# A graph layer on one core: the first block's outer products in two fp32r parts, other rings of buffers, gelu's table loaded at another place

## The chip, the cores and the metric

The kernel runs on one core of a Trainium2 chip. The core has five engines that run side by side, each through its own list of instructions in order: TensorE (PE in the profile; its weight loads are PEld), VectorE (DVE), ScalarE (ACT), GpSimd (POOL) and SyncE (SP), which here only issues transfers. They wait for each other by semaphores. On-chip memory is SBUF, matmuls add up in PSUM, and the DMA engines move data between SBUF and the memory outside (DRAM). The metric is the device time of one execution in microseconds (us), lower is better, as the median of several runs.

## The reference

There are 625 nodes with 512 features and 20,625 edges (10,000 in both directions, and a loop at each node), sorted by destination. An edge has a source, a destination, one of four relation types and a weight.

```python
h   = relu(layernorm(x))
msg = sum over r: (h[src] @ W_rel[r] + b_rel[r]) * (weight where type == r, else 0)
agg = segment_sum(msg, dst) / max(segment_sum(weight, dst), 1)
x1  = layernorm(h + h @ W_self + b_self + agg) * g1 + b1
ffn = gelu(x1 @ W_ffn1 + b_ffn1) @ W_ffn2 + b_ffn2      # 512 -> 1024 -> 512
out = x + layernorm(x1 + ffn) * g2 + b2
```

All inputs are fp32.

## The kernel before

**Tiles.** The nodes, padded to 640, form five blocks of 128. The edges form 162 tiles of 128. As edges are sorted by destination, a tile's edges fall in one block, or in two where blocks meet; `EdgePlan` works out which, with bounds that hold for nearly every graph. Edges outside of those bounds are counted (`count_outside`), and a branch at the end repeats the work in another way if there are any.

**First stage.** For each relation r and block i, `table_rows` multiplies the normalized block by `W_rel[r]` (L199), VectorE adds the bias (L202), and the rows are written to a table in DRAM, 2,560 rows in all. `later_loads` brings the other weights. VectorE prepares columns of the edge list and one-hot tiles for the degree sums (`degree_hots`). The order of TensorE, VectorE and ScalarE in this stage is the one written.

**Gathered tiles.** After that stage `edge_tile` handles the 132 tiles that touch blocks 1 to 4. GpSimd gathers the 128 table rows of the tile's edges into `ms` (L484). ScalarE multiplies them by the weights and rounds to the type fp32r, which gives `hi` (L489); VectorE computes the rest, `lo` (L491). TensorE multiplies each by a one-hot of the destinations and adds them up in PSUM (L507, L508): two matmuls of type fp32r in place of one in fp32. A one-hot tile serves four edge tiles (L503). `ms` has a ring of `MS = 13` buffers, `hi` and `lo` one of three each.

**First block.** The 36 tiles that touch block 0 gather nothing. `first_sums` takes two at a time. A one-hot `os` of the source's row in its chunk (L285) is multiplied, as an outer product over the tile's edges, by `od`: a matrix that holds the edge's weight in the column of its destination and chunk (L291, compare and multiply in one instruction). L300 adds the products up in PSUM banks, in fp32, 58 products of 20 to 420 columns; when a bank is complete, ScalarE copies it to `sums_w` (L305). `first_products` then multiplies these sums by the table itself: SyncE loads it in 20 chunks of 128 rows, `tr` (L363), and L374 multiplies, two chunks a step. `tr` uses the same ring as `ms`, and a load is issued `LA = 4` chunks ahead.

**Degree, self part, norm, feed-forward.** `degree_sums` adds up the weights of each node, `degree_end` inverts them and sends them through DRAM to turn them into columns (`rdeg`), with two transfers on SP's queue. `self_part` is `h @ W_self` of a block (L210), kept in DRAM too. When a block's sum is complete, `first_norm` runs on VectorE, the block is transposed by TensorE (L180), `up` multiplies by `W_ffn1` in eight pieces with gelu on ScalarE (L401, L403), `down` multiplies by `W_ffn2` (L409), and the second norm and the store follow.

**Order.** From the second stage on, TensorE's order comes from a planner in the program: it keeps a clock of its own, places a gathered tile whenever one is due (the first at 7.5 us, then one each 1.33), and between them takes the offered step of lowest rank whose due time has come: degree sums 0, the first block's work 1, other self parts 2, a transpose 9, feed-forward 10. Each step carries an estimated length; a transpose is due 9 us after its block's norm has been placed. The order on the other engines is left to the scheduler. `total_outside` is the matmul that adds up the count of edges outside (L249) and the copy of the count (L250).

Of the kernel before, what the change touches and what calls it, by code (L numbers as in the profile page):

```python
# [42 lines left out]
def gnn_layer(ctx, tc, x, edges, w_self, w_rel, w_ffn1, w_ffn2, rows_in, bf1_in, out, n_edges):  # L43
# [89 lines left out]
    ones = const.tile([P, 1], F32, name="ones")  # L133
    nc.vector.memset(ones, 1.0)
    half = const.tile([P, 1], F32, name="half")
    nc.vector.memset(half, -0.5)
# [129 lines left out]
    def first_columns():  # L266
# [11 lines left out]
                                       op0=ALU.mult, op1=ALU.add)  # L278

    bank = {}  # L280

    def first_sums(j0, n):

        oh = work.tile([P, 2, P], F32, tag="os", name=f"os_{j0}")
        nc.vector.tensor_tensor(oh[:, :n, :], key[:, 0, j0:j0 + n].unsqueeze(2).to_broadcast([P, n, P]),  # L285
                                node_row[:, :P].unsqueeze(1).to_broadcast([P, n, P]), op=ALU.is_equal)
        for j in range(j0, j0 + n):
            lo, hi = ep.window[j]
            hi = min(hi, P)
            ow = work.tile([P, NW * NC], F32, tag="od", name=f"od_{j}", bufs=3)  # L290
            nc.vector.tensor_scalar(ow[:, :(hi - lo) * NC], key_row[:, :(hi - lo) * NC], key[:, 1, j:j + 1],  # L291
                                    wgt[:, j:j + 1], op0=ALU.is_equal, op1=ALU.mult)
            for q in range(lo // BW, (hi - 1) // BW + 1):
# [6 lines left out]
                nc.tensor.matmul(bank[q][:, (a - q * BW) * NC:(z_ - q * BW) * NC], oh[:, j - j0, :],  # L300
                                 ow[:, (a - lo) * NC:(z_ - lo) * NC],
                                 start=False, stop=(j == meets[-1]))
                if j == meets[-1]:
# [75 lines left out]
    def first_norm(b, agg, pool_pow=False):  # L379
        zi = z[:, b, :]  # L380
        nc.vector.scalar_tensor_tensor(zi, agg, rdeg[:, b:b + 1], zi, op0=ALU.mult, op1=ALU.add)
        mean, t = variance(zi, f"z{b}")
        a = work.tile([P, D], F32, tag="hn", name=f"za_{b}")
        nc.vector.scalar_tensor_tensor(a, zi, mean, g1_bc, op0=ALU.subtract, op1=ALU.mult)
        rstd = rsqrt_pow(t, True) if pool_pow else rsqrt_scaled(t)
        x1 = work.tile([P, D], F32, tag="x1", name=f"x1_{b}")
        nc.vector.scalar_tensor_tensor(x1, a, rstd, b1_bc, op0=ALU.mult, op1=ALU.add)
# [4 lines left out]
    def feed_forward(blocks, x1T, gT, pool_pow=False):  # L392
# [12 lines left out]
        def down(i, f):  # L405
# [5 lines left out]
            if f + 2 < KF:  # L411
                return
            y = work.tile([P, D], F32, tag="y", name=f"y_{i}")
            nc.vector.tensor_add(y, po[i], z[:, i, :])
            mean, t = variance(y, f"y{i}")
            a = work.tile([P, D], F32, tag="hn", name=f"ya_{i}")
            nc.vector.scalar_tensor_tensor(a, y, mean, g2_bc, op0=ALU.subtract, op1=ALU.mult)
# [13 lines left out]
    DG = 27  # L431
    MS = 13
    LA = 4
    chunks = [(j0, min(DG, NT - j0)) for j0 in range(0, NT, DG)]
    groups = [(j0, min(2, n_first - j0)) for j0 in range(0, n_first, 2)]
    with tc.manual_schedule(engines={PE, DVE, ACT}):
# [13 lines left out]
        for r in range(R):  # L450
            for i in range(NB):
# [21 lines left out]
    with tc.manual_schedule(engines={PE}):  # L473
# [7 lines left out]
        def edge_tile(j):  # L481
# [5 lines left out]
            w = wgt[:, j:j + 1]  # L487
            hi = edge.tile([P, D], F32R, tag="hi", name=f"hi_{j}")
            nc.scalar.activation(hi, ms, AF.Copy, scale=w)  # L489
            lo = edge.tile([P, D], F32R, tag="lo", name=f"lo_{j}")  # L490
            nc.vector.scalar_tensor_tensor(lo, ms, w, hi.bitcast(F32), op0=ALU.mult, op1=ALU.subtract)  # L491
# [42 lines left out]
        def norm_and_feed(b):  # L534
# [13 lines left out]

            offer(9, now + 9.0, [(0.7, 0.0, turned)])

# [25 lines left out]
        while left or steps:  # L576
# [18 lines left out]
    with tc.If(some_out > 0):  # L595
# [4 lines left out]
        with tc.For_i(0, NT, 1) as j:  # L600
# [4 lines left out]
            nc.vector.tensor_copy(gw[:, 1:2], wgt[:, bass.ds(j, 1)])  # L605
            gm = work.tile([P, D], F32, tag="y", name="gm")
            nc.gpsimd.indirect_dma_start(
# [57 lines left out]
```

## Time and profile before

| | |
|---|---|
| runs | 330.9, 331.29, 334.62 us; median 331.29 |
| profiled execution | 366.07 us, of which the span between its first and last instruction is 364.2 |
| TensorE's granted clock, mean | 0.929 |
| TensorE busy | 301.1 us, 83% of the span |
| VectorE busy | 229.0 us, 63% |
| GpSimd busy | 153.1 us, 42% |
| ScalarE busy | 120.9 us, 33% |
| moved by DMA | 61.71 MB, 169 GB/s over the span |

A profile comes from one execution, and this one took longer than the plain runs. Times in it are microseconds from the span's start. "Busy" counts an engine's instructions; a matmul's end is modelled and overlaps the next one, so that the distance from start to start tells more of TensorE than the length of one. An fp32 matmul leaves two records, one of type fp32r leaves one, and both are printed with the output's type f32. In a group of instructions, "idle before" is the time for which the engine stood still ahead of them, with what released it. The chain of waits is followed back from the last instruction, at each step to what released it.

### The profile page before, as it was taken

How to read it: one execution, taken by the hardware profiler on the slowest of the kernel's cores; microseconds unless marked ns; L12 is line 12 of the kernel's file. 1: busy time of each engine (PE TensorE's matmuls, PEld its weight loads, DVE VectorE, ACT ScalarE, POOL GpSimd, SP SyncE). 2: the span in 40 equal slices, each digit the busy share in tenths (PEclk: the TensorE clock that was granted, in tenths of full speed). 3: DMA queues.
4: the chain of work that ended last, by engine and by line, in shares of the span. 5: the costliest groups of instructions: out<-in, count | busy, mean ns of one | idle time of the engine just before them, and what ended most of it. 6: DMA issues, size and time to landing. Idle time of an engine off the chain costs nothing.

```text
span 364.2 us, 4077 instructions
## 1 busy us (share of the span) xinstructions
PE 301.1 (83%) x1264; PEld 191.1 (52%) x1266; DVE 229.0 (63%) x470; ACT 120.9 (33%) x195; POOL 153.1 (42%) x224
## 2 busy tenths in 40 slices
PE   1799999997847599999988947398989975999990
PEld 0344444445523468775544426285776665687750
DVE  2324767995623579998675561398757866786503
ACT  2230000000330345653433432364545525562210
POOL 5100000001777437743444777367757774301001
PEclk9999999999878599999989997699998996999997
DMA  7989852121877455575688667355656674400000
GB/s 281 413 298 335 281 190 86 58 86 61 167 198 253 142 163 147 170 225 161 213 302 282 174 200 202 94 150 173 185 158 187 174 207 124 146 2 30 6 28 27
DMA packets 24556, 61.71 MB, mean 169 GB/s; under 512 B 4577, under 2 KB 4577, under 8 KB 24274
## 3 DMA queue, kind: packets, MB, share of 16 engines
q0 software_dynamic: 10560, 34.61, 33.2%
q1 hardware_dynamic: 13968, 26.79, 20.8%
q8 instruction: 12, 0.20, 0.2%
q14 instruction: 14, 0.11, 0.1%
q10 hardware_dynamic: 2, 0.00, 0.0%
HBM read 53.55 MB, written 7.84 MB: 169 GB/s over the span
## 4 chain that ended last, share of the span: by engine, by line
PE 58%; issue 11%; DMA 9%; DVE 8%; another core or an unknown queue 5%; ACT 5%; POOL 2%; SPq 0%; POOLq 0%; ACTq 0%; DVEq 0%
PE pt L199 19%; PE po L409 8%; PE pu L401 7%; PE acc L508 7%; PE acc L507 6%; DMA ms<-table,row_i 6%; PE bank L300 5%; PE pz L210 4%; ACT hi L489 4%; DVE lo L491 4%; POOL ms L484 2%; DMA xs<-in_x_dram 2%; PE acc L374 1%; DMA table<-m 1%
## 5 line engine op out<-in xcount | busy, mean ns | idle before, releaser
L484 POOL DMA_INDIRECT ms<-table,row_i x132 | 143.3, 1085 | 151.2 <-issue 91.2
L489 ACT ACTIVATE hi<-ms,ed 128x512 fp32r<-128x512 f32 x132 | 92.5, 719 | 157.8 <-DMA ms<-table,row_i 95.4
L491 DVE SCALAR_TENSOR_TENSOR lo<-ms,ed,hi 128x512 fp32r<-128x512 f32 x132 | 96.9, 747 | 58.6 <-ACT hi L489 36.4
L507 PE MATMUL acc<-hi,oh 128*128 128x512 f32 x150 | 80.1, 534 | 19.9 <-issue 10.7
L199 PE MATMUL pt<-wr,hT 128*128 128x512 f32 x160 | 71.0, 603 | 0.0
L508 PE MATMUL acc<-lo,oh 128*128 128x512 f32 x150 | 64.9, 432 | 6.1 <-DVE lo L491 5.6
L401 PE MATMUL pu<-x1T,w_sb 128*128 128x128 f32 x320 | 44.7, 289 | 7.2 <-issue 6.5
L199 PEld LDWEIGHTS pt<-wr,hT 128*128 128x128 f32 x160 | 30.8, 195 | 37.4 <-issue 36.9
L401 PEld LDWEIGHTS pu<-x1T,w_sb 128*128 128x128 f32 x320 | 44.3, 205 | 10.8 <-issue 6.9
L507 PEld LDWEIGHTS acc<-hi,oh 128*128 128x128 f32 x150 | 30.5, 203 | 33.9 <-issue 18.6
L508 PEld LDWEIGHTS acc<-lo,oh 128*128 128x128 f32 x150 | 30.4, 202 | 24.3 <-DVE lo L491 13.8
L409 PE MATMUL po<-w_sb,gT 128*128 128x512 f32 x80 | 36.6, 592 | 0.0
L503 DVE TENSOR_TENSOR oh<-fl,node_row 128x512 fp32r<-128x512 f32 (+2 forms) x39 | 25.5, 666 | 8.3 <-DMA table<-m 3.2
L202 DVE TENSOR_TENSOR m<-pt,brel_bc 128x512 f32<-128x512 f32 x20 | 13.7, 688 | 23.2 <-PE pt L199 23.2
L300 PE MATMUL bank<-od,os 128*128 128x60 f32 (+19 forms) x116 | 27.0, 369 | 0.6 <-issue 0.6
L403 ACT ACTIVATE gT<-pu,bf 128x128 f32<-128x128 f32 x40 | 14.7, 367 | 36.6 <-PE pu L401 15.5
L300 PEld LDWEIGHTS bank<-od,os 128*128 128x128 f32 x116 | 21.6, 214 | 4.5 <-issue 0.9
L409 PEld LDWEIGHTS po<-w_sb,gT 128*128 128x128 f32 x80 | 14.9, 189 | 13.4 <-issue 12.5
L374 PE MATMUL acc<-tr,sums_w 128*128 128x512 f32 x40 | 20.0, 625 | 0.0
L210 PE MATMUL pz<-ws_sb,hT 128*128 128x512 f32 x40 | 19.2, 624 | 0.0
L291 DVE TENSOR_SCALAR od<-key_row,key,ed 128x400 f32<-128x400 f32 (+15 forms) x36 | 15.7, 443 | 0.8 <-PE bank L300 0.8
L210 PEld LDWEIGHTS pz<-ws_sb,hT 128*128 128x128 f32 x40 | 8.4, 211 | 8.2 <-issue 7.8
(94 smaller groups left out, 161.9 us busy)
## 6 DMA issues: line engine op xcount, KB each, us to landing
table<-m SPq DMA_DIRECT2D x20, 256.0 KB
tr<-table SPq DMA_DIRECT2D x20, 256.0 KB
wr<-in_L_gnn_W_rel_dram SPq DMA_DIRECT2D x4, 1024.0 KB
w_sb<-in_L_gnn_W_ffn_dram SPq DMA_DIRECT2D x2, 2048.0 KB
ms<-table,row_i POOLq DMA_INDIRECT x132
rows<-in_rows_dram SPq DMA_DIRECT2D x1, 1536.0 KB
z_kept<-z SPq DMA_DIRECT2D x5, 256.0 KB
xs<-in_x_dram SPq DMA_DIRECT2D x2, 512.0 KB
```

The lines of the kernel that those rows point to most:

```text
L199: nc.tensor.matmul(p, hT[:, k, i * P:(i + 1) * P], wr_sb[r][:, k, :], start=(k == 0), stop=(k == KD - 1))
L210: nc.tensor.matmul(p, hT[:, k, i * P:(i + 1) * P], ws_sb[:, k, :], start=(k == 0), stop=(k == KD - 1))
L300: nc.tensor.matmul(bank[q][:, (a - q * BW) * NC:(z_ - q * BW) * NC], oh[:, j - j0, :], ow[:, (a - lo) * NC:(z_ - lo) * NC], start=False, s ...
L374: nc.tensor.matmul(acc[0], sums_w[:, c_, :], chunks_[c_], start=(c_ == 0), stop=(c_ == NC - 1))
L401: nc.tensor.matmul(pu[:, :nn], w1_sb[:, k, f * P:(f + 1) * P], x1T[:, k, n0:n0 + nn], start=(k == 0), stop=(k == KD - 1))
L409: nc.tensor.matmul(po[i], g[:, f_, i * P - n0:(i + 1) * P - n0], w2_sb[:, f_, :], start=(f_ == 0), stop=(f_ == KF - 1))
L484: nc.gpsimd.indirect_dma_start(out=ms, out_offset=None, in_=table[:, :], in_offset=bass.IndirectOffsetOnAxis(ap=row_i[:, j:j + 1], axis=0))
L489: nc.scalar.activation(hi, ms, AF.Copy, scale=w)
L491: nc.vector.scalar_tensor_tensor(lo, ms, w, hi.bitcast(F32), op0=ALU.mult, op1=ALU.subtract)
L503: nc.vector.tensor_tensor(ohs[b][:, :ng, :], dst_f[:, j:j + ng].unsqueeze(2).to_broadcast([P, ng, P]), node_row[:, b * P:(b + 1) * P].unsq ...
L507: nc.tensor.matmul(acc[b], oh, hi, start=first, stop=False)
L508: nc.tensor.matmul(acc[b], oh, lo, start=False, stop=end)
```

## The change

- **Outer products.** `os` is multiplied by the weights in place of `od`. The weight is split into an fp32r part and the rest (`first_weights`, two small instructions on VectorE in the first stage). ScalarE scales each `os` tile by either part into `ohw` (two activations of 128 columns for each of the 36 tiles, 72 in all), `od` is a comparison alone, written as fp32r, and each product becomes two fp32r matmuls, one for each part, into the same bank. `ohw` and `od` share the ring of six that the degree one-hots (`oc`) had.
- **Rings.** `MS` goes from 13 to 7, `hi` gets five buffers and `lo` four. `tr` has a ring of its own with three buffers, and `LA` goes from 4 to 3. The tiles of both norms move to the ring of six of the degree stage's `ow`.
- **gelu's table.** An activation of one column with Gelu is placed in the first stage, after relation 0, and brings the table load with it.
- **Planner.** The transfer that brings `rdeg` and the count of edges outside (`total_outside`) are steps of their own, due at 14 us of the planner's clock. The transposes of all blocks but the last are due 15 us after the norm, not 9.

In the order of the built program the count's matmul leaves the head of TensorE's second stage and comes behind seven gathered tiles; the outer products have fewer gathered tiles and one self part fewer between them, and these follow later. On SP the first three `tr` loads stand ahead of the two degree transfers and the stores of the self part.

```diff
+    w2 = const.tile([P, 2, n_first], F32R, name="w2")
+
+    def first_weights():
+        nc.vector.tensor_copy(w2[:, 0, :], wgt[:, :n_first])
+        nc.vector.tensor_sub(w2[:, 1, :], wgt[:, :n_first], w2[:, 0, :].bitcast(F32))
...
         oh = work.tile([P, 2, P], F32, tag="os", name=f"os_{j0}")
+        ohw = work.tile([P, 2, 2, P], F32R, tag="oc", name=f"ohw_{j0}", bufs=6)
...
-            ow = work.tile([P, NW * NC], F32, tag="od", name=f"od_{j}", bufs=3)
+            for part in range(2):
+                nc.scalar.activation(ohw[:, j - j0, part, :], oh[:, j - j0, :], AF.Copy,
+                                     scale=w2[:, part, j:j + 1].bitcast(F32))
+            ow = work.tile([P, NW * NC], F32R, tag="oc", name=f"od_{j}", bufs=6)
             nc.vector.tensor_scalar(ow[:, :(hi - lo) * NC], key_row[:, :(hi - lo) * NC], key[:, 1, j:j + 1],
-                                    wgt[:, j:j + 1], op0=ALU.is_equal, op1=ALU.mult)
+                                    None, op0=ALU.is_equal)
...
-                nc.tensor.matmul(bank[q][:, (a - q * BW) * NC:(z_ - q * BW) * NC], oh[:, j - j0, :],
-                                 ow[:, (a - lo) * NC:(z_ - lo) * NC],
-                                 start=False, stop=(j == meets[-1]))
+                for part in range(2):
+                    nc.tensor.matmul(bank[q][:, (a - q * BW) * NC:(z_ - q * BW) * NC], ohw[:, j - j0, part, :],
+                                     ow[:, (a - lo) * NC:(z_ - lo) * NC],
+                                     start=False, stop=(j == meets[-1] and part == 1))
...
         nc.sync.dma_start(deg_dram.rearrange("(a c) -> c a", c=C), dg[:, 0, :])
+
+    def degree_rows():
         nc.sync.dma_start(rdeg, deg_dram.rearrange("(b p) -> p b", p=P))
...
-            tr = edge.tile([P, D], F32, tag="ms", name=f"tr_{c}", bufs=MS)
+            tr = edge.tile([P, D], F32, tag="tr", name=f"tr_{c}", bufs=LA)
...
-    MS = 13
-    LA = 4
+    MS = 7
+    HL = 5
+    LA = 3
...
                 if r == 0 and i == NB - 1:
+                    nc.scalar.activation(gelu_of, ones, AF.Gelu)
                     first_columns()
+                    first_weights()
...
-            hi = edge.tile([P, D], F32R, tag="hi", name=f"hi_{j}")
+            hi = edge.tile([P, D], F32R, tag="hi", name=f"hi_{j}", bufs=HL)
...
-            lo = edge.tile([P, D], F32R, tag="lo", name=f"lo_{j}")
+            lo = edge.tile([P, D], F32R, tag="lo", name=f"lo_{j}", bufs=HL - 1)
...
-            offer(9, now + 9.0, [(0.7, 0.0, turned)])
+            offer(9, now + (9.0 if last else 15.0), [(0.7, 0.0, turned)])
...
+        offer(-1, 14.0, [(0.0, 0.0, degree_rows), (0.2, 0.0, total_outside)])
...
                     degree_end(pdeg)
-                    total_outside()
                     did = True
```

More of the change, by code (lines that the diff above doesn't have):

```diff
@@ L134, in gnn_layer @@
     nc.vector.memset(ones, 1.0)
+    gelu_of = const.tile([P, 1], F32, name="gelu_of")
     half = const.tile([P, 1], F32, name="half")
@@ L382, in first_norm @@
         mean, t = variance(zi, f"z{b}")
-        a = work.tile([P, D], F32, tag="hn", name=f"za_{b}")
+        a = work.tile([P, D], F32, tag="ow", name=f"za_{b}", bufs=6)
         nc.vector.scalar_tensor_tensor(a, zi, mean, g1_bc, op0=ALU.subtract, op1=ALU.mult)
         rstd = rsqrt_pow(t, True) if pool_pow else rsqrt_scaled(t)
-        x1 = work.tile([P, D], F32, tag="x1", name=f"x1_{b}")
+        x1 = work.tile([P, D], F32, tag="ow", name=f"x1_{b}", bufs=6)
         nc.vector.scalar_tensor_tensor(x1, a, rstd, b1_bc, op0=ALU.mult, op1=ALU.add)
@@ L412, in down @@
                 return
-            y = work.tile([P, D], F32, tag="y", name=f"y_{i}")
+            y = work.tile([P, D], F32, tag="ow", name=f"y_{i}", bufs=6)
             nc.vector.tensor_add(y, po[i], z[:, i, :])
             mean, t = variance(y, f"y{i}")
-            a = work.tile([P, D], F32, tag="hn", name=f"ya_{i}")
+            a = work.tile([P, D], F32, tag="ow", name=f"ya_{i}", bufs=6)
             nc.vector.scalar_tensor_tensor(a, y, mean, g2_bc, op0=ALU.subtract, op1=ALU.mult)
@@ L605, in gnn_layer @@
             nc.vector.tensor_copy(gw[:, 1:2], wgt[:, bass.ds(j, 1)])
-            gm = work.tile([P, D], F32, tag="y", name="gm")
+            gm = work.tile([P, D], F32, tag="ow", name="gm", bufs=6)
             nc.gpsimd.indirect_dma_start(
```

## The prediction

> **What bounds the kernel now.** I read the page's first two parts, then the chain of waits, then the waits by line, then three kinds of timeline around the lines that the change touches.
>
> ```profile
> PE 301.1 (83%) x1264; PEld 191.1 (52%) x1266; DVE 229.0 (63%) x470; ACT 120.9 (33%) x195; POOL 153.1 (42%) x224
> PE 58%; issue 11%; DMA 9%; DVE 8%; another core or an unknown queue 5%; ACT 5%; POOL 2%; SPq 0%; POOLq 0%; ACTq 0%; DVEq 0%
> PE pt L199 19%; PE po L409 8%; PE pu L401 7%; PE acc L508 7%; PE acc L507 6%; DMA ms<-table,row_i 6%; PE bank L300 5%; PE pz L210 4%; ACT hi L489 4%; DVE lo L491 4%; POOL ms L484 2%; DMA xs<-in_x_dram 2%; PE acc L374 1%; DMA table<-m 1%
> ```
>
> TensorE carries the chain: 58% of it is matmuls, and L300, the products that the change rewrites, is 5%. But an average hides stages. The engine table by stretch, at the end of the outer products:
>
> ```profile
> 134.00:144.00 10.00, 9.79 (x47) 7.53 (x46) 9.70 (x19) 6.53 (x10) 6.54 (x6) 1.00 0.44 131
> 144.00:154.00 10.00, 10.00 (x52) 8.13 (x51) 9.95 (x22) 6.03 (x9) 8.17 (x7) 1.00 0.57 165
> ```
>
> Columns: stretch, length, busy PE, PEld, DVE, ACT, POOL, clock, DMA share, GB/s. Two engines are full here: TensorE (10.00) and VectorE (9.95). That is the main difficulty. Elsewhere TensorE waits in a few places:
>
> ```profile
> DVE lo L491 <- ACT hi L489: 36.4, 32, 7.8
> PE acc L507 <- ACT hi L489: 8.7, 4, 6.7
> PE tp_x L180 <- DVE x L387: 7.7, 2, 5.9
> 222.28 1.28 ACT L403 ACT_TABLE_LOAD   x1
> 232.76 0.37 ACT L403 ACTIVATE gT<-pu,bf 128x128 f32<-128x128 f32 x1 [9.20 <-remote]
> ```
>
> gelu's table takes 1.28 us while TensorE is busy with feed-forward, and the first gelu then starts 9.20 us later for a reason that the trace doesn't name.
>
> The profiled execution took 366.07 us (span 364.2, so 1.9 around it), the median of the plain runs is 331.29: 35 us more. TensorE has gaps at 100.7, 115.7, 213.7, 226.8, 268.9 and 298.4 of some 2 to 7 us, about 31 us together, whose releasers are "issue", "unknown queue" or a late gather. Most of these can't be in the plain runs. I count changes on the profile and take their sum off the median.
>
> **What the Trainium skill says.** "ScalarE: Activation LUTs", What ACT_TABLE_LOAD costs: 1283 ns a load; an activation 186 ns + 0.833 ns per column, 93 ns more per pointer operand, neighbours overlapping by 93 ns. The trace agrees: 1.28 us, and hi of 512 columns 719 ns against 706. "VectorE: DVE Perf Modes", the perf-mode tier table: fp32 tensor_scalar runs at twice the rate of tensor_tensor; L291 shows it (400 columns 484 ns, 120 columns 330 ns: 0.55 ns a column). "DMA: Bandwidth & Descriptors", Anatomy of one DMA: 2.0 us + bytes/436 GB/s, so 2.6 us for 256 KB; the chain shows 2.97 us for a table write of that size. No page that I found prices an fp32r matmul by its width.
>
> **The change, part by part.**
>
> *TensorE's outer products.* The timeline gives what a pass costs:
>
> ```profile
> 97.67 0.39 PE L508 MATMUL acc<-lo,oh 128*128 128x512 f32 x1
> 97.89 0.39 PE L507 MATMUL acc<-hi,oh 128*128 128x512 f32 x1
> 98.12 0.39 PE L508 MATMUL acc<-lo,oh 128*128 128x512 f32 x1
> 150.12 1.57 PE L300 MATMUL bank<-od,os 128*128 128x300 f32 x8
> 151.39 0.52 PE L507 MATMUL acc<-hi,oh 128*128 128x512 f32 x1
> ```
>
> fp32r rows of 512 columns start 0.228 us apart: 0.44 ns a column. An fp32 product shows two records: the eight at 150.12 are four products of 300, 100, 220 and 180 columns, done in 1.27 us, 1.6 ns a column. So fp32 costs 3.6 times an fp32r pass, and two fp32r passes about half of it. There are 58 products with 11,080 columns; with a floor of 0.065 us a record (two of 20 columns at 149.43 are done in 0.14) fp32 comes to 19.2 us, two fp32r parts to 10.9: 8.3 us less. The trace shows no fp32r narrower than 512. Ends: 10.9, and some 21 if the 39 products under 256 columns ran four times slower per column. I take 10.9; the next paragraph says why the other end costs little.
>
> *The stretch of outer products.* From the built programs' order I count what lies between the seventh gathered tile and the last outer product. TensorE before: 56 products 18.7, two self parts at 3.43, 26 tiles at 0.456, zero fills 1.2: 38.7 us. After: 112 parts 10.6, one self part, 22 tiles, the same fills: 25.3 us. VectorE by start to start in the timeline (lo 0.66, od 0.40, os 0.34, oh 0.60): before 38.3, after 37.1 (dropping the multiply saves nothing at one column rate; if fp32r output lost the double rate, 32 x 0.15 = +5). ScalarE gains 60 scalings of 128 columns (12 more lie earlier), by the skill's price 0.386 us alone and 0.293 in a row: 17.6, plus 23 hi at 0.64 and 5.6 for bank copies: 38 us, from 22. So TensorE falls by 13 us and stops being the bound; ScalarE and VectorE, at 38 and 37, replace it, and fp32r's price up to 21 stays inside TensorE's slack. Before, the stretch ran from 108.95 to 161.1; without the 4.98 gap 47.2, part of it at a clock of 0.69 to 0.79, when TensorE was the slow one. After, with the coupling of three full engines, I take 43: **-4.2**. But one self part and four tile products are pushed behind the stretch, where TensorE sets the pace: 3.43 + 4 x 0.456 = **+5.3**. The parts of the change that should pay most nearly cancel.
>
> *The count of strays (pcnt) and the SP queue.* pcnt leaves TensorE's head, where it waited 2.47 us (L249). Seven tiles follow that are gated by gathers, 1.25 us apart on GpSimd and ready from 94.6 on, so the seventh is done near 103 either way: **0** (ends -2.5 and 0). On SP three table loads now pass ahead of the degree transfers and the store of z; they add 0.8 MB while the first gathers run, within a rate of 225 GB/s in 100 to 120 against 413 reached earlier: 0. rdeg is needed only after 178.
>
> *Own ring for the first block's table rows, three deep.* Before, the ten steps of L374 ran from 178.40 to 211.15: 3.28 us each, where two products (1.72) and two tiles (0.92) make 2.64; 6.4 us lost, since the shared ring held gathers back (GpSimd waited 9.63 us at 169.79) and hi came late. After, load c+3 waits for product c; the odd one is needed 2.64 us later and lands after 0.32 + 2.97 = 3.29: 0.65 x 9 = 5.9 us lost. **-0.5**. Ends: +14 with landings as slow as the gathers' 5.38 in the chain there, -6 if the wait hides.
>
> *Rings of 7, 5 and 4.* A gather needs about 4.2 us to land (88.95 to 93.11) and 1.5 to be split; at 1.3 us a tile five slots suffice, seven hold. The deeper hi and lo meet the waits above: TensorE's on hi and lo come to 8.7 + 5.6 us, 6.7 of it one of the gaps; I take **-3** of the rest (ends 0 and -7).
>
> *gelu's table early.* ScalarE is idle for 66.68 us ahead of its first hi at 93.11, which hides the 1.28 us. If only the load goes, -1.3; with the silence of 9.20 behind it, -10.5. The plain runs lack most such silences: **-4**.
>
> *Later transposes.* The wait of 1.82 us at 250.06 goes; that at 304 lies in a gap: **-1.8**. The shared six slots for za, x1, y cost nothing, two each sufficed.
>
> Sum: -4.2 + 5.3 - 0.5 - 3 - 4 - 1.8 = -8.2; 331.29 - 8.2 = **323**.
>
> **The rivals.** *No measurable change* (2% is about what a measurement of this kernel can tell from none): ScalarE and VectorE never overlap better than 46 us in the stretch, and the table is worth its 1.28 alone: -1.2, +5.3, -0.5, -3, -1.3, -1.8 give 329. For it: both engines are full in the table above. *Slower by the three-deep ring*: each load waits for the product three before it. If landings take 5 to 5.4 us under the gathers' traffic (the DMA share is 0.85 from 178 to 200), nine steps lose 2.4 to 3 us each, 15 to 21 over my count: 338 to 344, say 340. It decides from a landing of 4.9 us. Against: table writes take 2.97. *Slower by ScalarE in the stretch*: four scalings stand before each hi and wait for slots that TensorE frees two groups later (six slots, three a group); hi, lo and tiles queue behind. If a third of ScalarE's time is lost so, 38 becomes 57, and with the coupling up to 61: +14 to +18, 339. Against: the slots are two groups ahead. *The change not doing what it says*: narrow fp32r at fp32's cost; hidden by the slack, it is the second case.
>
> **How the numbers follow.** Forecast 0.50, no change 0.22, the ring 0.14, ScalarE 0.14. The forecast's own range is 312 to 325: the table at -10.5 and hi and lo at -7 give 312. The slow cases reach 341. I leave out a tenth at either end: 312 to 341. Faster by over 2% (under 324.7) 0.50, within 0.22, slower 0.28.
>
> **What would show it.** L300 at some 10 to 12 us start to start; in the stretch ScalarE near 90% and TensorE below 70%; L374 every 3.2 to 3.4 us with waits on tr; no 9 us silence before gelu; fewer waits for hi. It is wrong if the stretch is longer than 47 us, if L374's steps exceed 4 us, or if gaps on an unknown queue grow or vanish wholesale.

## The result, and the profile after

The changed kernel takes 331.04 us (median of 20 runs, 327.64 to 338.16); the kernel before beside it 331.88 (20 runs, 330.2 to 334.62). The ratio is 0.9967, 95% interval [0.9943, 0.9992]: a third of a per cent, where 2.5% were forecast. The runs below fall into five groups, each with its own runs of the kernel before; in the first two that kernel takes 330 to 331 us (the short groups, "e1" and "e2"), in the last three 362 to 365 (the long groups, "e3" to "e5"), so every ratio is to the kernel before of its own group. Each group ran on a chip of its own (12 and 4 the short, 1, 13 and 15 the long), so that chip and hour can't be told apart here. The profile that the prediction was read from, 366 us, is like those of the long groups.

The changed kernel's page: busy time of each engine, and its chain by engine and by line.

```profile
PE 286.3 (88%) x1266; PEld 179.7 (55%) x1266; DVE 226.7 (70%) x472; ACT 139.2 (43%) x268; POOL 153.1 (47%) x224
...
PE 68%; DMA 14%; ACT 9%; DVE 4%; issue 2%; POOL 1%; SPq 0%; POOLq 0%; ACTq 0%; DVEq 0%
PE pt L200 22%; PE po L424 11%; PE pu L416 10%; PE acc L526 8%; PE acc L525 8%; DMA tr<-table 6%; DMA ms<-table,row_i 5%; ACT ohw L300 5%; PE pz L211 4%; PE acc L389 3%; ACT hi L507 3%; DMA xs<-in_x_dram 2%; DVE lo L509 1%; ACT sums_w L318 1%; PE tp_h L181 1%
```

The share of an unknown queue (5%) is gone and "issue" is down from 11% to 2%. That is no work of the change: the kernel before, profiled in a short group (run e1_before, span 328.2), has no such queue in its chain, 4% of "issue", and after 90 us no idle stretch over 1.4 us put down to either on TensorE, VectorE or ScalarE, where the profile used for the forecast has ten, 55 us over the three engines. New on the chain are "DMA tr<-table", 6%, and the scalings at L300, 5%. The engine table of the changed kernel for the stretches shown before:

```profile
134.00:144.00 10.00, 8.25 (x47) 6.58 (x46) 9.54 (x22) 10.00 (x27) 6.75 (x6) 1.00 0.58 159
144.00:154.00 10.00, 9.65 (x40) 6.35 (x41) 8.06 (x16) 8.51 (x17) 7.48 (x7) 1.00 0.63 178
```

In the first of them ScalarE (fourth busy figure) has risen from 6.53 to 10.00 of 10 us and stands where TensorE (first) stood; in the second the outer products end at 146.7, so it shows less of them than it did before. And the waits by line, in us in all, times, and longest, the last line from e1_before:

```profile
DVE lo L509 <- ACT hi L507: 27.0, 31, 4.9
...
PE acc L525 <- ACT hi L507: 7.2, 3, 4.1
...
PE acc L389 <- DMA tr<-table: 6.3, 8, 1.8
```
```profile
PE acc L507 <- ACT hi L489: 7.1, 5, 5.0
```

TensorE's waits for hi are what they were in the clean trace of the kernel before (7.1), and those for table rows are new: 6.3 us.

### The profile page after: what moved, and what is told of

Same layout as the page of the kernel before. It is cut to its first block, busy times and chain, and to the rows that moved or that the text cites. A ratio compares the mean times of both kernels' runs of the same rounds, so it can differ in the third digit from the quotient of the medians.

```text
span 325.8 us, 4193 instructions
## 1 busy us (share of the span) xinstructions
PE 286.3 (88%) x1266; PEld 179.7 (55%) x1266; DVE 226.7 (70%) x472; ACT 139.2 (43%) x268; POOL 153.1 (47%) x224
## 4 chain that ended last, share of the span: by engine, by line
PE 68%; DMA 14%; ACT 9%; DVE 4%; issue 2%; POOL 1%; SPq 0%; POOLq 0%; ACTq 0%; DVEq 0%
PE pt L200 22%; PE po L424 11%; PE pu L416 10%; PE acc L526 8%; PE acc L525 8%; DMA tr<-table 6%; DMA ms<-table,row_i 5%; ACT ohw L300 5%; PE pz L211 4%; PE acc L389 3%; ACT hi L507 3%; DMA xs<-in_x_dram 2%; DVE lo L509 1%; ACT sums_w L318 1%; PE tp_h L181 1%
## 5 line engine op out<-in xcount | busy, mean ns | idle before, releaser
L502 POOL DMA_INDIRECT ms<-table,row_i x132 | 143.2, 1085 | 124.2 <-DVE oh L521 69.2
L525 PE MATMUL acc<-hi,oh 128*128 128x512 f32 x150 | 75.6, 504 | 7.2 <-ACT hi L507 7.2
L526 PE MATMUL acc<-lo,oh 128*128 128x512 f32 x150 | 62.5, 417 | 2.6 <-DVE lo L509 2.5
L300 ACT ACTIVATE ohw<-os,w 128x128 fp32r<-128x128 f32 x72 | 23.2, 398 | 58.4 <-PE pdeg L356 58.2
L416 PEld LDWEIGHTS pu<-x1T,w_sb 128*128 128x128 f32 x320 | 40.6, 191 | 4.9 <-ACT gT L418 1.4
L416 PE MATMUL pu<-x1T,w_sb 128*128 128x128 f32 x320 | 41.2, 275 | 1.7 <-ACT gT L418 1.0
L525 PEld LDWEIGHTS acc<-hi,oh 128*128 128x128 f32 x150 | 29.3, 195 | 18.4 <-ACT hi L507 9.5
L389 PE MATMUL acc<-tr,sums_w 128*128 128x512 f32 x40 | 22.0, 644 | 6.4 <-DMA tr<-table 6.3
L521 DVE TENSOR_TENSOR oh<-fl,node_row 128x512 fp32r<-128x512 f32 (+2 forms) x39 | 25.7, 662 | 1.0 <-issue 1.0
L313 PEld LDWEIGHTS bank<-od,ohw 128*128 128x128 f32 x116 | 18.1, 202 | 6.5 <-issue 2.8
L313 PE MATMUL bank<-od,ohw 128*128 128x60 f32 (+19 forms) x116 | 20.3, 308 | 1.5 <-DVE od L303 0.8
L211 PE MATMUL pz<-ws_sb,hT 128*128 128x512 f32 x40 | 18.9, 617 | 0.0
L389 PEld LDWEIGHTS acc<-tr,sums_w 128*128 128x128 f32 x40 | 6.8, 195 | 15.9 <-DMA tr<-table 14.4
```

Of the source, the lines that this page charges most:

```text
L211: nc.tensor.matmul(p, hT[:, k, i * P:(i + 1) * P], ws_sb[:, k, :], start=(k == 0), stop=(k == KD - 1))
L300: nc.scalar.activation(ohw[:, j - j0, part, :], oh[:, j - j0, :], AF.Copy, scale=w2[:, part, j:j + 1].bitcast(F32))
L389: nc.tensor.matmul(acc[0], sums_w[:, c_, :], chunks_[c_], start=(c_ == 0), stop=(c_ == NC - 1))
L416: nc.tensor.matmul(pu[:, :nn], w1_sb[:, k, f * P:(f + 1) * P], x1T[:, k, n0:n0 + nn], start=(k == 0), stop=(k == KD - 1))
L502: nc.gpsimd.indirect_dma_start(out=ms, out_offset=None, in_=table[:, :], in_offset=bass.IndirectOffsetOnAxis(ap=row_i[:, j:j + 1], axis=0))
L525: nc.tensor.matmul(acc[b], oh, hi, start=first, stop=False)
```

## The experiments

**The kernel before, with a clean trace.** No edit.

> The kernel before, profiled once more, for a trace without the gaps of the first one (31 us on an unknown queue or on nothing named). If the forecast had the stages right, the stretch from the seventh gathered tile to the last outer product takes 46 to 48 us here against 39 in the changed kernel, and the ten steps of the first block's products 33 to 34 us against 37.2: the gain is made and partly given back. The rival: the stretch is already near 40 us without the gaps, so there was no gain to give back.

It took 330.06. The engine table of this run by stages: the outer products from the seventh gathered tile on, from there to the first product with table rows, from there to the first feed-forward product, and the rest.

```profile
107.40:152.10 44.70, 44.06 (x189) 32.01 (x189) 40.14 (x82) 22.96 (x34) 35.26 (x32) 0.95 0.72 218
152.10:169.30 17.20, 15.94 (x52) 9.38 (x52) 13.29 (x21) 8.81 (x14) 4.65 (x4) 1.00 0.64 200
169.30:204.00 34.70, 29.84 (x88) 15.30 (x86) 24.39 (x46) 15.54 (x22) 23.44 (x23) 1.00 0.83 260
204.00:328.20 124.20, 111.24 (x572) 81.30 (x572) 87.91 (x193) 60.75 (x109) 69.66 (x65) 0.98 0.50 144
```

The same four stages of the changed kernel:

```profile
107.70:146.70 39.00, 35.60 (x174) 26.79 (x174) 35.44 (x77) 35.59 (x88) 25.98 (x23) 0.91 0.64 190
146.70:162.40 15.70, 15.41 (x53) 9.85 (x54) 12.65 (x19) 10.16 (x16) 12.15 (x12) 1.00 0.68 196
162.40:206.70 44.30, 37.91 (x108) 19.49 (x107) 29.64 (x62) 18.39 (x28) 28.15 (x28) 0.96 0.81 270
206.70:325.80 119.10, 108.07 (x569) 80.56 (x568) 86.08 (x183) 57.10 (x106) 65.17 (x63) 0.99 0.50 144
```

The first stage starts 0.3 us later, then: -5.7, -1.5, +9.6, -5.1, together -2.4, the difference of the spans. So the stretch of outer products is shorter, as forecast, but 5.3 of its 5.7 us are a self part and four tile products that left it, and the third stage gives it all back. That stage holds a self part (3.43) and six tile products (2.74) more than before, the four pushed out and two that the last stage no longer has. The other 3.4 us are a balance: TensorE's new waits for table rows, 6.3 us, less its waits for hi, lo and the transpose, 4.9 us there in the kernel before, and matmul records with table rows that are stretched themselves (up to 1.12 us in place of 0.59).

**The outer products alone.** The kernel before with this (and the split of the weights into w2):

```
-            ow = work.tile([P, NW * NC], F32, tag="od", name=f"od_{j}", bufs=3)
+            for part in range(2):
+                nc.scalar.activation(ohw[:, j - j0, part, :], oh[:, j - j0, :], AF.Copy,
+                                     scale=w2[:, part, j:j + 1].bitcast(F32))
+            ow = work.tile([P, NW * NC], F32R, tag="oc", name=f"od_{j}", bufs=6)
...
+                for part in range(2):
+                    nc.tensor.matmul(..., ohw[:, j - j0, part, :], ...)
```

> The kernel before with the outer products alone changed: two fp32r parts, scaled on ScalarE, everything else as it was. If the stretch gives what the forecast counted (4 us, with the order of the tiles left as it was, so that nothing is pushed behind it), 325 to 328 us, ratio 0.98 to 0.99. If ScalarE and VectorE overlap no better than TensorE did, ratio 0.997 to 1.005. If the scalings hold up the split of gathered rows, above 1.01.

Measured: 328.94 us, ratio 0.9986 [0.9958, 1.0014]. By this ratio no gain can be told from none. The medians of all runs, 328.94 and 330.88, are 1.9 us apart, so a gain of that size isn't excluded. Its first stage takes 43.1 us against 44.7, at the same order of tiles: VectorE is busy 38.68 of them and ScalarE, with 22.96 before, 38.16. The price of a part is in the changed kernel's timeline, first its matmuls, then the weight loads of the same place:

```profile
136.54 1.07 PE L313 MATMUL bank<-od,ohw 128*128 128x300 f32 x8
137.45 0.42 PE L525 MATMUL acc<-hi,oh 128*128 128x512 f32 x1
```
```profile
136.31 1.13 PEld L313 LDWEIGHTS bank<-od,ohw 128*128 128x128 f32 x8
```

Eight parts, the same 800 columns as in the four fp32 products that took 1.27 us before, start to start 0.91: 0.72 of the time, not the 0.55 counted. Their eight weight loads take 1.13 us. Over the stretch, start to start and without named waits, 112 records cost 16.6 us; 112 of fp32 in e1_before cost 18.9. Each part loads weights of its own, and the loads of successive parts start at least 0.108 us apart. 39 of the 58 products are under 256 columns, 0.11 us at 0.44 ns a column, too narrow to cover a load. Narrow parts in a row show the pace: these six, of 40, 40, 60, 60, 20 and 20 columns, start 0.11 us apart from the second on, whatever their width.

```profile
145.73 0.87 PEld L313 LDWEIGHTS bank<-od,ohw 128*128 128x128 f32 x6
145.96 0.73 PE L313 MATMUL bank<-od,ohw 128*128 128x40 f32 x6
```

The Trainium skill, "TensorE: Matmul & The Clock Gate", LDWEIGHTS (loading the stationary operand), prices a load by its columns alone, 107 ns for 128; the 108 ns between loads here agree. At the larger of 0.112 us and 0.44 ns a column the 112 parts come to 13.8 us, an estimate from these figures. Of the 2.8 us above it, 1.3 fall on ten parts at a granted clock of 0.50 (109.3 to 112.5 us of the trace, 2.4 us); the rest isn't explained, and may be waits for ScalarE's scalings that the modelled ends hide. The fp32 products have as many loads, 116 on both pages, but at 1.6 ns a column most of them are wide enough to cover theirs.

**gelu's table alone.**

```
+                    nc.scalar.activation(gelu_of, ones, AF.Gelu)
                     first_columns()
```

> The kernel before with gelu's table loaded early and nothing else. The forecast counted 4 us for it: about 328, ratio 0.988. If only the load of 1.28 us counts, ratio 0.996; if ScalarE has room for the load at the old place, 1.000.

Measured: 331.74 us, ratio 1.0017 [0.9985, 1.0049]: nothing. ScalarE's timeline in e1_before shows why:

```profile
204.08 0.72 ACT L489 ACTIVATE hi<-ms,ed 128x512 fp32r<-128x512 f32 x1 [0.16 <-DMA ms<-table,row_i]
204.82 1.28 ACT L403 ACT_TABLE_LOAD   x1
206.12 0.37 ACT L403 ACTIVATE gT<-pu,bf 128x128 f32<-128x128 f32 x1
```

The load takes its 1.28 us and the first gelu follows at once. There is no silence of 9.20 us.

What the silence was can be found in the first profile. On TensorE, around the same time:

```profile
226.00 1.05 PE L401 MATMUL pu<-x1T,w_sb 128*128 128x128 f32 x8
233.79 0.79 PE L507 MATMUL acc<-hi,oh 128*128 128x512 f32 x1 [6.74 <-ACT hi L489]
```

The trace also holds the time at which each semaphore was updated. TensorE's eight matmuls of L401 end at 227.05 by the trace; its semaphore shows no update from 224.31 to 232.74, then eight within 0.35 us, and the gelu starts at 232.76. So ScalarE waited for TensorE's late signal (or for matmuls that ended later than the model of the trace has it), and not for the table. All eleven traces of long executions (the first profile and those of the long groups) have 42 to 88 updates of TensorE's semaphore over 0.1 us behind any matmul's end; the other nine have two, at the very end. The eleven are also incomplete: they hold 1,644 to 2,292 records of semaphore updates by transfers, the nine 3,169 or 3,170. This can be seen on a page, which then has no landing times. The gathers' line of the first profile, and of e1_before (median 3.8 us):

```profile
ms<-table,row_i POOLq DMA_INDIRECT x132
```
```profile
ms<-table,row_i POOLq DMA_INDIRECT x132, 3.8
```

A releaser called "issue" or "unknown queue" on such a page can be a missing record. Why the signals come late, and whether the recording that loses records also slows the program, isn't shown.

**Five slots for table rows in the changed kernel.**

```
-    LA = 3
+    LA = 5
```

> The changed kernel with the ring for the first block's table rows five deep in place of three. If the three-deep ring gives the gain back (20 us of landings on the chain, of which the steps lose some 9 us against 2.64 each), the ten steps fall from 37 to 28 to 31 us and the kernel takes 322 to 326, ratio to before 0.975 to 0.985. If the landings are slow because the DMA engines are full (share 0.87 to 0.93 there), deeper loads only queue: steps stay at 36 to 37, ratio 0.995 to 1.0.

Measured: 321.6 us, ratio 0.9755 [0.9697, 0.9813], some 9 us under both kernels. TensorE's 40 records with table rows (two to a product; duration, then first and last start) in the kernel before, the changed one, and this one:

```profile
L374 PE MATMUL acc<-tr,sums_w x40: 590/592/593, 169.3 to 199.9; 128*128 128x512 f32 x40
```
```profile
L389 PE MATMUL acc<-tr,sums_w x40: 590/592/1123, 162.4 to 198.2; 128*128 128x512 f32 x40
...
DMA to landing us min/median/max: 2.7/4.2/5.3
```
```profile
L389 PE MATMUL acc<-tr,sums_w x40: 590/592/697, 162.6 to 188.3; 128*128 128x512 f32 x40
...
DMA to landing us min/median/max: 2.8/5.2/6.1
```

30.6, 35.8 and 25.7 us from the first start to the last; the steps, start to start, are 3.3, 3.8 and 2.7 us on average, where 2.64 is what TensorE alone needs. With five slots the loads land later than with three (5.2 us at the median against 4.2) and yet are hardly waited for: it is slots that hide a landing, not its speed. Of the 10 us gained here over the changed kernel 7 are left at the end (spans of 325.8 and 318.8).

**Rings of their own in the kernel before.** Two runs with otherwise untouched code, three and five slots:

```
-            tr = edge.tile([P, D], F32, tag="ms", name=f"tr_{c}", bufs=MS)
+            tr = edge.tile([P, D], F32, tag="tr", name=f"tr_{c}", bufs=LA)
...
-    MS = 13
-    LA = 4
+    MS = 10
+    LA = 3
```

(with MS = 8, LA = 5 in the second).

> The kernel before with one edit: the first block's table rows get a ring of their own of three slots, and the gathers keep ten of the thirteen. If three slots are what lost the changed kernel its gain, the steps go from 3.2 us to 3.7 and the time up by some 5 us: 335 to 337, ratio 1.012 to 1.02. If the loss comes from the company that the loads have in the changed kernel (more gathers under way, because hi and lo are freed sooner), the steps stay near 3.2 and the ratio at 1.00.

> The kernel before with a ring of five slots of their own for the first block's table rows, eight for the gathers. If the depth of that ring is worth the same without the rest of the change, the steps fall from 3.2 to 2.7 us: 325 to 327, ratio 0.982 to 0.990. If the deep ring only pays beside the other edits, 0.997 to 1.003.

Measured: three slots 330.6 us, ratio 1.0021 [0.9990, 1.0053]; five 322.31, 0.9767 [0.9693, 0.9841], more than expected. The same line of the two runs:

```profile
L374 PE MATMUL acc<-tr,sums_w x40: 592/592/697, 169.3 to 204.3; 128*128 128x512 f32 x40
```
```profile
L374 PE MATMUL acc<-tr,sums_w x40: 592/592/697, 167.7 to 194.8; 128*128 128x512 f32 x40
```

The first run is neither of the two expectations: its products did go up, from 30.6 to 35.0 us, and yet the time did not. What pays it back, by the traces, is GpSimd, which the shared ring had held up. Its waits in e1_before, and the engine table of 147 to 173 us there (the fifth busy figure is GpSimd):

```profile
POOL ms L484 <- DVE lo L491: 17.8, 21, 8.0
...
POOL ms L484 <- PE acc L374: 2.6, 3, 1.8
```
```profile
147.00:160.00 13.00, 12.49 (x56) 8.82 (x55) 11.03 (x21) 6.11 (x10) 4.83 (x4) 1.00 0.74 235
160.00:173.00 13.00, 12.25 (x40) 6.89 (x39) 9.80 (x17) 6.16 (x9) 6.83 (x6) 1.00 0.62 184
```

The same with a ring of three:

```profile
147.00:160.00 13.00, 12.49 (x56) 8.83 (x55) 11.04 (x21) 6.15 (x10) 10.56 (x9) 1.00 0.64 172
160.00:173.00 13.00, 11.48 (x37) 6.04 (x35) 9.78 (x17) 6.84 (x11) 9.04 (x9) 1.00 0.72 212
```

Four and six gathers started in those stretches become eight and eight (a count in the lines can hold one that was already running); by 180 us 61 have started instead of 55, and the part from the first feed-forward product on is 121.6 us long instead of 124.2. With five slots the kernel gets both: gathers that run on (60 started by 180 us), and products that hardly wait (27.1 us). This one edit to the kernel before is worth as much as the five-slot version of the whole change, and both are faster than the two kernels compared here.

**The split's rings and the fp32 products, undone at five slots.** In the five-slot version of the changed kernel, hi and lo at three slots each; and, in another run, first_sums as before (one fp32 product, the weight multiplied on VectorE).

```
-            hi = edge.tile([P, D], F32R, tag="hi", name=f"hi_{j}", bufs=HL)
+            hi = edge.tile([P, D], F32R, tag="hi", name=f"hi_{j}", bufs=3)
...
-            lo = edge.tile([P, D], F32R, tag="lo", name=f"lo_{j}", bufs=HL - 1)
+            lo = edge.tile([P, D], F32R, tag="lo", name=f"lo_{j}", bufs=3)
```

> The changed kernel with a five-deep ring for table rows (321.6 us in its run), and the rings of hi and lo back at three each, as before. If the deeper hi and lo rings are worth the 3 us that the forecast gave them, 324 to 325.5, ratio to before 0.983 to 0.986. If they only shift where ScalarE and VectorE wait, 321 to 322.5, ratio 0.972 to 0.977.

> The changed kernel with a five-deep ring for table rows and the outer products back in one fp32 pass, the weight multiplied in on VectorE: no scalings on ScalarE. If the two fp32r parts are worth the 4 us of the forecast in this order of the work, 325 to 326, ratio 0.983 to 0.988. If the stretch is set by VectorE and the rows' arrival and not by TensorE, 320 to 322.5, ratio 0.97 to 0.977; if the scalings are a burden, below 320.

Measured: 323.7 us, ratio 0.9775 [0.9687, 0.9864], and 323.3, 0.9785 [0.9689, 0.9880], against 0.9755 [0.9697, 0.9813]. Neither can be told from the five-slot kernel, but the intervals are wide enough to hide the 3 or 4 us of the forecast. In the fp32 run the outer products' stage, in the changed kernel's order of tiles, takes 41.0 us (104.7 to 145.7), in the five-slot kernel 42.1 (104.8 to 146.9): in these two traces the two parts buy no time.

**The two smallest edits, undone one by one.** In the changed kernel: hi and lo at three slots, as above; and the transposes due as before,

```
-            offer(9, now + (9.0 if last else 15.0), [(0.7, 0.0, turned)])
+            offer(9, now + 9.0, [(0.7, 0.0, turned)])
```

> The changed kernel with the rings of hi and lo at three each, as before. The forecast gave the deeper rings 3 us (ends 0 and 7): then 334, ratio to before 1.005 to 1.010. If the gathers' pace on GpSimd sets the end, what counts is whether a gathered row's slot comes free later: 331 to 333, ratio 0.998 to 1.004.

> The changed kernel with the transposes due 9 us after a block's norm, as before, in place of 15. The forecast gave the later transposes 1.8 us: then 332.8, ratio 1.002. If the wait is made up by TensorE's slack behind the gathers, 331, ratio 0.995 to 0.999. The two are hardly apart; a ratio over 1.006 would be a larger effect than either.

These fell into a long group: 344.75 us, ratio 0.9502 [0.9442, 0.9563], and 346.65, 0.9564 [0.9502, 0.9626], where the kernel before took 361.96. Neither expectation covers that, and the group lacked the changed kernel as a measure. It was run in the next group, beside a kernel with both edits undone:

> The changed kernel once more, beside the runs that follow. Where the kernel before takes some 330 us, ratio 0.993 to 1.000 as before. Where it takes 362, as in the runs just made: if stalls that come whatever the kernel does add a fixed amount to both, 0.995; if the changed kernel's edits shorten what those stalls hold up, 0.95 to 0.96, as its two near relatives showed there (0.950 and 0.956).

> The changed kernel with hi and lo in three slots each and the transposes due after 9 us, both as before. The forecast gave these two edits 3 and 1.8 us: then 4.8 us over the changed kernel, ratio to it 1.0145. If the gathers' pace sets the end, so that neither edit is on the path, within 1.5 us of the changed kernel, ratio to it 0.997 to 1.005.

The changed kernel: 342.8 us against 364.71, ratio 0.9436 [0.9351, 0.9521]. Where the kernel before takes 365 us, the change makes it 5.6% faster. With both edits undone 348.59, 0.9566 [0.9508, 0.9625]: 5.8 us more at the medians, 4.7 by the ratios, where the forecast gave the two 4.8; the two intervals overlap at their ends, and the early transposes alone (0.9564, in the group before) stand where both edits undone stand. TensorE's wait for the transpose, which the late due time is to avoid, is there in this run's timeline; VectorE's lines, from just before it, show why it is so long:

```profile
234.68 1.12 PE L181 MATMUL tp_x<-ident,x 128*128 128x128 f32 x4 [8.58 <-DVE x L402]
```
```profile
228.91 0.75 DVE L509 SCALAR_TENSOR_TENSOR lo<-ms,ed,hi 128x512 fp32r<-128x512 f32 x1 [3.35 <-ACT hi L507]
232.49 0.69 DVE L521 TENSOR_TENSOR oh<-fl,node_row 128x512 fp32r<-128x512 f32 x1 [2.70 <-remote]
```

VectorE, which makes the block that is transposed, lost 6 us of the 8.58 to waits of its own, the second with no releaser named. In e1_before TensorE's longest wait of this kind is 1.8 us. So what the two edits bring in a long group may be in part slack for its stalls.

**gelu's table, once more.** The edit as above, in a long group.

> The kernel before with gelu's table loaded early alone, once more. Where the kernel before takes 362 to 365 us, as it did in the two batches just before, and its trace has a silence of 9.20 us behind the table load: if that silence belongs to the load, 4 to 10 us less, ratio 0.973 to 0.989; if it is a stall that comes of itself, which the load only happened to precede, 0.995 to 1.005. Where the kernel before takes 330, 1.000 again.

Measured: 359.38 us, ratio 0.9887 [0.9797, 0.9976]: 4.1 us less, with the interval from 0.9 to 7.4, from five runs and barely clear of none. It lies at the upper edge of what I expected if the silence belonged to the load, but the first profile shows that silence behind TensorE's late signal; how the early load would bring 4 us isn't shown. Where the kernel takes 330 us the term is not there.

**What sets the end at five slots.** The last gather starts 39 to 40 us before the end in the kernel before, in the changed one and with five slots, so I suspected the gathers' pace on GpSimd. Two ways to load GpSimd alone, and two to relieve TensorE:

```
             w = wgt[:, j:j + 1]
+            nc.gpsimd.memset(pad, 0.0)
```

> The changed kernel with five slots for table rows, and a memset of one column on GpSimd after each of the 132 gathers: 0.09 us of its time each, 12 us in all, and no other engine's. If the gathers' pace on GpSimd sets the end there (in its trace the last gather starts 39.6 us before the end, and GpSimd waits for slots for only 9 us), 329 to 334 against 321.6, ratio to before 0.997 to 1.012. If TensorE sets the end, 321 to 323, ratio 0.975 to 0.980.

```
+            nc.gpsimd.memset(ms[:, 0:1], 0.0)
             nc.gpsimd.indirect_dma_start(
```

> The changed kernel with five slots for table rows, and ahead of each of the 132 gathers a memset of one column of its slot on GpSimd, some 0.1 to 0.2 us each: 12 to 26 us of GpSimd's time and no other engine's. (The run before with a memset put them all at the start of the program, where they cost nothing.) If the gathers' pace on GpSimd sets the end, the time rises by most of that, less GpSimd's 9 us of waiting: ratio to the five-slot kernel 1.015 to 1.05. If TensorE sets it, below 1.006.

```
-        offer(1, 0.0, sums_left + selfs[:2] + rest + [(0.0, 0.0, lambda: norm_and_feed(0))])
-        offer(2, 0.0, selfs[2:])
+        sums_left = sums_left[:7] + selfs[1:2] + sums_left[7:11] + selfs[0:1] + sums_left[11:15] + selfs[2:3] + sums_left[15:]
+        offer(1, 0.0, sums_left + rest + [(0.0, 0.0, lambda: norm_and_feed(0))])
+        offer(2, 0.0, selfs[3:])
```

> The changed kernel with five slots for table rows, and three of the self parts placed among the outer products, where TensorE has 7 us of gaps, in place of one: the other two self parts' 6.9 us leave the part behind. If TensorE sets the end, 315 to 318, ratio 0.955 to 0.963. If the gathers' pace does, 320 to 323, ratio 0.970 to 0.979, with TensorE waiting for tiles later on.

```
-        sums_left = [(0.6 + 0.5 * (j0 > 8), 0.3, lambda j0=j0, n=n: first_sums(j0, n)) for j0, n in groups]
+        sums_left = [(0.5, 0.9, lambda j0=j0, n=n: first_sums(j0, n)) for j0, n in groups]
```

> The changed kernel with five slots for table rows, and the planner's cost of a group of outer products set to 0.5 us with a wait of 0.9, so that two self parts more stand among the first outer products and gathered tiles, where TensorE waits for slow gathers, and two fewer behind the stretch. If TensorE sets the end, 6.9 us less than the five-slot kernel: ratio to it 0.978 to 0.985. If the gathers' pace does, ratio to it 0.995 to 1.005.

And their measure, the five-slot kernel in a long group:

> The changed kernel with five slots for table rows, once more, as the measure for the slower gather and the early self parts. Where the kernel before takes 362 to 365: if the gathers' pace on GpSimd sets the end, the slower gather (0.926) lies 0.015 or more above it, so 0.91 or less, and the early self parts (0.929) at or above it. If TensorE sets the end, it lies 0.015 to 0.02 above the early self parts, at 0.945. If neither does alone, 0.92 to 0.935. Where the kernel before takes 330, 0.972 to 0.980 again.

Measured, all in long groups: the five-slot kernel 335.1 us, ratio 0.9264 [0.9204, 0.9325]. Slower gathers: the first form put all its memsets ahead of the gathers, between 5.9 and 29.6 us, so it loads the start only (341.6, 0.9395, the first tile 4 us later); the second 337.9, 0.9257 [0.9172, 0.9341], with 14.7 us of memsets. Gathers, memsets and the idle time between them come to 210.2 us there against 203.9 without, 6 us more and not 15: GpSimd's idle time shrinks by 5.5 us, since a memset can fall where it waits before a gather anyway, and the gathers themselves take 2.9 us less.

Self parts inside: 341.35, 0.9402 [0.9334, 0.9470]; its outer products end at 171.4 us in place of 146.2, because later groups stand behind the self parts. Self parts early: 336.64, 0.9292 [0.9216, 0.9368]; the trace has one self part more in the stretch (at 117.7 in place of 147.3), not two, and the outer products end at 150.9, 4.7 us later.

If GpSimd alone set the end, its 6 us would be a ratio of 0.943, outside the interval of the second slower form, so that suspicion fails. If TensorE did, two self parts less would be 0.907. But in both of these runs the outer products end later, by 25.2 and 4.7 us, so neither shows TensorE relieved, and of TensorE they say little. All this is of long groups; in the short ones it wasn't tried, and what sets the end stays open.

## Why the prediction was wrong

The step that failed is the one that I took before any of the terms: "I count changes on the profile and take their sum off the median". The profile was of an execution of 366 us and the median of 331. I wrote of the 31 us of gaps that "most of these can't be in the plain runs", and yet kept part of them as terms of the change: 8.8 us for gelu's table, the deeper rings and the later transposes. In executions of 330 us the runs show nothing for the table (+0.6 us, interval -0.5 to +1.6) and, by the estimate under 2, at most some 1.6 us for all three behind the first feed-forward product.

1. *gelu's table, -4.* Failed. I kept 4 of the 10.5 us; alone it is worth nothing in a short group. In a long one it came to 4.1 us, but the silence that I read as its price was TensorE's late signal.
2. *Rings of 7, 5 and 4, -3, and later transposes, -1.8.* Read off waits of the same execution (6.7 us of one gap, 1.82 us at 250.06). In a long group they are worth 5.8 us at the medians. In the short groups they weren't measured on the changed kernel itself. A bound by difference, an estimate: its rest after the first feed-forward product is 5.1 us shorter, 0.9 of it two tile products done earlier; a ring of three alone, without these edits, brings 2.6. At most some 1.6 us are left there for gelu's table and these two, where I had 8.8. What the deeper hi and lo brought ahead of that product isn't separated; at five slots they came to 0.7 us at the ratios, with intervals that could hide 3.
3. *Outer products on TensorE, 18.7 to 10.6 us in the stretch (19.2 to 10.9 in all).* The first figure was right (18.9), the second mis-sized: 16.6. The floor of 0.065 us a record came from fp32 products of 20 columns; narrow fp32r parts in a row start 0.11 us apart, the pace of their loads, and that alone turns the 10.6 into some 13.8 by the estimate above. I had said that slack would hide such a price, and it nearly does: ScalarE's busy time in the stretch is as long as TensorE's. The sign "TensorE below 70%" failed (91% of the stretch in the records), "ScalarE near 90%" held (35.6 of 39.0 us), "fewer waits for hi" failed.
4. *The stretch, -4.2, and +5.3 behind it.* Near in size: -5.7. It is 39.0 us against 43, and before 44.7 against the 47.2 that I had left after taking off one gap. But little of it is TensorE's saving: with the old order of tiles the same products save 1.6. The self part and four tile products that were merely pushed out, the same 5.3 us that I counted behind it, are nearly all. That the sum of the two is near what was forecast is in part luck, since the products themselves save far less than the 8.3 us that I counted for TensorE.
5. *Own ring of three slots, -0.5.* The net was near (+0.7 on the kernel before, interval -0.3 to +1.7), but by luck: two terms, both larger than mine, cancel. I took a landing of 3.29 us, from a table write of 256 KB; it was 4.2 at the median, with the gathers beside it (4.3 in the kernel before, whose deeper ring hid it), and the steps 3.8, not 3.2 to 3.4. I had also read the steps before as 3.28 us by taking the start of the last matmul for the end; start to start they were 3.5 in that profile. Against that, gathers no longer held by the shared ring came out earlier than I counted. I named the danger as a rival at 340, deciding from 4.9 us; the landing stayed below at the median.
6. *pcnt and SP's queue, 0.* Right: the seventh tile starts at 107.7 against 107.4.

Without gelu's term and the 4.8 of point 2 the sum is +0.6, and 331.9 the forecast. The rival that came nearest, no measurable change at 329, had the verdict and only half of the reason: the stretch did go below 46 us, and the table was worth not even 1.28. My last sign had it: wrong "if gaps on an unknown queue grow or vanish wholesale". They vanished.

In the long groups the change is worth 5.6%. gelu's table and the two edits of point 2 would explain about 9 of the 21 us there; the traces place more in the outer products, 53.7 us in the prediction's profile against 40.2 in the changed kernel's of a long group (110.0 to 150.2). Which part brings that stays open. The stalls of the long groups go with late signals of TensorE; what delays those stays open too.

## What to carry to other kernels

Compare the profiled execution's own time with the median before reading a single wait: where they differ by 10%, a stall that the profile doesn't explain must not be booked as a term, not even in part. A page whose transfers have no landing times comes from an incomplete trace, and its unnamed releasers may be missing records. Where transfers share a ring with others, count slots by landing time over step time, and look for who else the ring holds up; here a three-line edit (five slots of their own for the table rows) gave 2.3% where the whole change gave 0.3%. And a product split into two cheaper passes still pays a weight load for each; where a pass is too narrow to cover its load, it saves less than its columns say.

## What the runs showed of the hardware that I had not expected

- The same program takes 330 us in some groups of runs and 362 to 365 in others, and the ratio of two kernels depends on it: 0.9967 and 0.9436 for the same pair. In every trace of a long execution 42 to 88 updates of TensorE's semaphore come late, often in bursts, against two in the others, and records of updates are missing.
- fp32r parts of 20 to 420 columns start 0.114 us apart in one place and 0.148 on average, where their weight loads start 0.108 apart at the least; parts of 300 columns start 0.13 apart.
- A plain load of 256 KB lands in 4.2 us at the median beside gathers, and in 5.2 with five under way; writes of that size took 2.1 in the same profile.
- Memsets of 0.11 us between the gathers, 14.7 us in all, made GpSimd's work 6 us longer; without them it stands idle for 0.30 us before most gathers.
